# Where a graph network's second weight block is combined: beside the edge counting, or after the first head

## The chip, the cores and the metric

The kernel runs on one core of a Trainium2 chip. The core has a matrix engine (TensorE, PE in the profile), a vector engine (VectorE, DVE), an activation engine (ScalarE, ACT), a general engine (GpSimd, POOL) and a queue that starts transfers (SyncE, SP). Each engine runs its own instructions strictly in its own order; semaphores tie the engines together. Time is device microseconds of one execution, and the number compared is the median over executions: before the change 3097.74 us over three (3096.92 to 3099.75).

## The reference, cut to what matters

The model is a chain of four blocks over 512 nodes of width 768. Each block adds a graph layer, a token mixer and a feed-forward part to the nodes. Only the start of the first block is touched here: a layer norm, a count of the edges, and a graph attention layer with eight heads.

```python
edge_index = jnp.stack([src, dst])            # 16384 edges between 512 nodes
xn = _layernorm(x, axis=-1)                   # 512 x 768
# first graph layer, head by head (8 heads of 768 columns)
h = (x @ W).reshape(n, H, C)                  # W1 is 768 x 6144
alpha_s = jnp.einsum('nhc,hc->nh', h, a_s)
alpha_d = jnp.einsum('nhc,hc->nh', h, a_d)
e = jax.nn.leaky_relu(alpha_s[src] + alpha_d[dst], NEG_SLOPE)
m = jax.ops.segment_max(e, dst, num_segments=n)
e = jnp.exp(e - m[dst])
denom = jax.ops.segment_sum(e, dst, num_segments=n)
alpha = e / (denom[dst] + EPS)
out = jax.ops.segment_sum(h[src] * alpha[:, :, None], dst, num_segments=n)
# blocks 2 and 3 of the chain use the degree of each node
deg = jax.ops.segment_sum(jnp.ones_like(dst), dst, num_segments=n)
```

The second graph layer multiplies the eight heads' outputs by W2 (6144 x 768); the kernel does this head by head, as "project".

## The kernel before the change

**The edge counting.** Instead of gathering along edges, the kernel counts how often each pair of nodes occurs, in a 512 x 512 matrix `cnt`. `edge_counts` is a generator of 128 steps; step j takes 128 edges, makes a one-hot row block for their sources (512 wide) and one for their destinations (256 wide, the upper half of the nodes marked by a factor 4096), and multiplies them on PE into two PSUM banks (line 708, two matmuls a step). The source block comes from DVE (line 704, one instruction) or from ACT (lines 701 and 702, two instructions): for j below 40 every odd step is ACT's, from 40 on every third. The destination block is always DVE's (line 705). Its input is a row of node numbers. Up to step 31 that row is `near`, a copy in PSUM in 32-bit numbers; from step 32 on it is `nodes`, in SBUF in 16-bit numbers. The one-hots live in a ring of 16 buffers, so step j waits for the matmuls of step j - 16. The 128 steps fall into five groups; at the end of a group, ACT (714), DVE (716 to 721) and POOL (722, 723) split the two banks into counts and add them into `cnt`.

**The products.** Large products use a seven-multiplication scheme (Strassen-Winograd) over halves of both operands. It needs sums of the left operand and differences of the weights. `SplitB` makes the weight differences on POOL: for each of three chunks four subtractions of 128 x 384 (lines 438 to 441), twelve in all, two of which (439) overwrite a quarter of the weights themselves. A product over three chunks (line 512 in the profile, 128 x 384) is the unit of PE work; a head takes fourteen. A 32-bit matmul stands as two records in the trace, so a product is a row of six.

**The head loop.** `heads(i)` loads the 768 columns of W1 for head i (three transfers of 768 KB, `split_weights`), combines them (`SplitB`), makes h = xn @ W1 and then the two node scores on DVE (line 796, four instructions each). In the first head the counting runs as a background: at each product's start `tick()` puts in seven steps. For head 1 the combining is `pinned`: it is written so that it stays behind everything issued before it on its engine. From head 1 on the background is the edge weighing of the head before (`weighing`: line 743 to 763, then transposes, line 787), so that its aggregation (line 901, PE) can follow the head's products. After the aggregation comes `project`, with a block of W2 that is also combined on POOL.

**Order.** A scheduler places the instructions on the engines by what is ready in its own model; `pinned` steps and data hold it back. Weight blocks alternate between two buffers, their differences between two `tw` buffers. All transfers go through the one SP queue in order.

**The degrees.** `degrees` adds up the rows of `cnt` (line 928, one DVE reduction over 2048 numbers), and takes an inverse square root with one correction step (lines 929 to 936, six small instructions on DVE and one on ACT). It is called after head 2's turn in the loop, but not pinned, and its first use is far behind.

Of the kernel before, what the change touches and what calls it, by code (L numbers as in the profile page):

```python
# [19 lines left out]
N = 512  # L20
D = 768
# [76 lines left out]
def kernel(ctx: ExitStack, tc: tile.TileContext, a: dict, out: bass.AP):  # L98
    nc = tc.nc
    V, S, G, T = nc.vector, nc.scalar, nc.gpsimd, nc.tensor  # L100
# [278 lines left out]
    HT = N // 2  # L379
# [45 lines left out]
    def ready(src):  # L425

        return SplitB(split_weights(src))
# [242 lines left out]
    def edge_counts(gp):  # L670

        HI, MAGIC = 4096.0, 1.5 * 2.0 ** 23
        nodes = gp.tile([P, N], HF, name="nodes")
        G.iota(nodes, pattern=[[1, N]], base=0, channel_multiplier=0,
               allow_small_or_imprecise_dtypes=True)
        near = psum()[:, :HT]
        V.tensor_copy(near, nodes[:, :HT])
        part = gp.tile([P, 1], FP, name="part")  # L680
        G.memset(part, -31.0 / 64.0)
        ef = gp.tile([P, 2, EC], FP, name="ef")
        V.tensor_copy(ef, edges)
        neg = gp.tile([P, EC], FP, name="neg")
        V.tensor_scalar(neg, ef[:, 0, :], -1.0, None, op0=ALU.mult)
        far = gp.tile([P, EC], FP, name="far")
        V.tensor_scalar(far, ef[:, 1, :], float(HT), None, op0=ALU.is_ge)
        V.scalar_tensor_tensor(ef[:, 1, :], far, -float(HT), ef[:, 1, :], op0=ALU.mult, op1=ALU.add)
        V.tensor_scalar(far, far, HI - 1.0, 1.0, op0=ALU.mult, op1=ALU.add)
        hots = []  # L690
        for _ in range(2):
            b = big_tile("oh").bitcast(BF)
            hots += [b[:, i * (N + HT) : (i + 1) * (N + HT)] for i in range(8)]
        n_groups = -(-EC // 26)
        for g in range(n_groups):
            js = range(EC * g // n_groups, EC * (g + 1) // n_groups)
            acc = [psum() for _ in range(2)]
            for j in js:
                oh = hots[j % len(hots)]
                if (j % 2 if j < 40 else j % 3 == 2):  # L700
                    S.activation(oh[:, :N], nodes, AF.Abs, bias=neg[:, j : j + 1])
                    S.activation(oh[:, :N], oh[:, :N], AF.Relu, bias=1.0, scale=-1.0)
                else:
                    V.tensor_scalar(oh[:, :N], nodes, ef[:, 0, j : j + 1], None, op0=ALU.is_equal)
                V.tensor_scalar(oh[:, N:], near if j < 32 else nodes[:, :HT], ef[:, 1, j : j + 1], far[:, j : j + 1],
                                op0=ALU.is_equal, op1=ALU.mult)
                for u in range(2):
                    T.matmul(acc[u], oh[:, N + u * P : N + (u + 1) * P], oh[:, :N],
                             start=j == js[0], stop=j == js[-1])
                yield  # L710
            for u in range(2):
                low, high = cnt[:, u, :], cnt[:, 2 + u, :]
                t = gp.tile([P, N], FP, name="up_t", bufs=2)
                S.activation(t, acc[u], AF.Identity, bias=part, scale=1.0 / HI)
                if g == 0:
                    V.tensor_scalar(high, t, MAGIC, -MAGIC, op0=ALU.add, op1=ALU.add)
                    V.scalar_tensor_tensor(low, high, -HI, acc[u], op0=ALU.mult, op1=ALU.add)
                else:
                    V.tensor_scalar(t, t, MAGIC, -MAGIC, op0=ALU.add, op1=ALU.add)
                    r = gp.tile([P, N], FP, name="up_r", bufs=1)  # L720
                    V.scalar_tensor_tensor(r, t, -HI, acc[u], op0=ALU.mult, op1=ALU.add)
                    G.tensor_add(high, high, t)
                    G.tensor_add(low, low, r)
        for t in range(NT):
            S.activation(off[:, t, :], cnt[:, t, :], AF.Relu, bias=bigc, scale=-BIG)
        nc.sync.dma_start(cnt_dram, cnt)
# [89 lines left out]

    open_products()

    def heads(i):
        w1 = split_weights(a["L0_gnn_W1"][:, i * D : (i + 1) * D])  # L820
        B = pinned(lambda: SplitB(w1)) if i == 1 else SplitB(w1)
        h = token_major("h")
        strassen_token(xs, B, lambda t, c, ps: S.copy(h[:, t, ts(c, HC)], ps), None,
                       None if i else n0.rest)
        flush()
        return h, node_scores(h, row(f"g0_as{i}"), gp), node_scores(h, row(f"g0_ad{i}"), gp)

    with tc.tile_pool(name="graph", bufs=1) as gp:
        counting = edge_counts(gp)
        for _ in range(24):  # L830
            next(counting)
        n0 = Norm(x, "xn", 1e-5)
        for t in (0, 2, 1, 3):
            n0.chunk(t)
            if t == 1:
                n0.first()
        xs = n0.split
        raw_xn = tc.dram_tile([P, NT, D], FP, name="raw_xn")
        nc.sync.dma_start(raw_xn, n0.n)
        for _ in range(16):  # L840
            next(counting)
        background.append(several(counting, 7))
        loose.append(background[0])
        head0 = heads(0)
        drain()
# [46 lines left out]
    with tc.tile_pool(name="gat0", bufs=2) as gp:  # L892
        h2 = token_major("h2")

        def aggregate(i, h, wT, norm=None):
            gT = feature_major("gT")
            sums = SplitA(gT, G, False)
            for n, f in enumerate((0, 3, 1, 4, 2, 5)):
                ps = psum()
                for s in range(NT):  # L900
                    T.matmul(ps, h[:, s, ts(f, P)], wT[:, s, :], start=s == 0, stop=s == NT - 1)  # L901
                elu(gT[:, f, :], ps, col("g0_b1", i * KC + f))
                if norm and n < NT:
                    norm.chunk(n)
                if f >= KC // 2:
                    sums.sums(f - KC // 2)
            return sums

        def project(i, sums):
            first = set()  # L910

            def add(t, j, ps):
                d = h2[:, t, ts(j, HC)]
                if i == 0 and (t, j) not in first:
                    first.add((t, j))
                    evacuate(d, ps)
                else:
                    V.tensor_add(d, d, ps)

            strassen_add(sums, ready(a["L0_gnn_W2"][i * D : (i + 1) * D, :]), add)  # L920
            flush()


        dinv = const.tile([P, NT], FP, name="dinv")

        def degrees():
            deg = tiny(NT, name="deg")
            V.tensor_reduce(deg, cnt, AX.X, ALU.add)
            V.tensor_scalar(deg, deg, 1.0, None, op0=ALU.add)
            S.activation(dinv, deg, AF.Sqrt)  # L930
            V.reciprocal(dinv, dinv)
            nw = tiny(NT, name="ln_nw4")
            V.tensor_mul(nw, dinv, dinv)
            V.tensor_mul(nw, nw, deg)
            V.tensor_scalar(nw, nw, -0.5, 1.5, op0=ALU.mult, op1=ALU.add)
            V.tensor_mul(dinv, dinv, nw)

        done = None
        for i in range(9):
            if done:  # L940
                g, hg, ew = done
                wT = gp.tile([P, NT, N], FP, tag="edge_wT", name="edge_wT", bufs=wt_bufs[0])
                if i < 8:
                    if i == 1:
                        background.append(delayed(5, weighing(ew, s4, d4, cnt, off)))
                    background.append(delayed(0 if i == 1 else 8, turned(ew, wT)))
                else:
                    for _ in turned(ew, wT):
                        pass
            if i < 8:  # L950
                h, s4, d4 = heads(i) if i else head0
                drain()
            if done:
                norm = performer_norm() if i == 8 else None
                sums = aggregate(g, hg, wT, norm)
            if i < 8:
                done = i, h, edge_weights(s4, d4, gp, cnt, off) if i else weight_tile(gp)
            else:
                ys, va = performer_values(norm)
            if i:  # L960
                project(g, sums)
            if i == 2:
                degrees()
        x = load_x()
        qT = last_gat(h2, "g0_as", "g0_ad", gp, cnt, off, lambda: performer_features(ys, 0))
        add_row_to(x, row("g0_b2"))
# [903 lines left out]
    with tc.tile_pool(name="ffn3", bufs=1) as fp:  # L1870
# [83 lines left out]
        for g in range(2):  # L1954
            wa = weights(a["L3_ffn_w2a"][g * N : (g + 1) * N, :])
            wb = weights(a["L3_ffn_w2b"][g * N // 2 : (g + 1) * N // 2, :], HD)
            for i in range(2):
                j = 2 * g + i
# [94 lines left out]
```

## Time and profile before

| | us |
|---|---|
| median of 3 executions | 3097.74 (3096.92 to 3099.75) |
| the profiled execution | 3099.04 |
| its span, first to last instruction | 3097.2 |
| PE busy | 3005.4 (97%) |
| DVE busy | 1482.7 (48%) |
| POOL busy | 1436.3 (46%) |
| ACT busy | 749.7 (24%) |
| mean granted clock of TensorE | 0.992 |

The span is 1.8 us short of the profiled execution's own time, and that execution is 1.3 us above the median. PE is busy nearly all the time, so what a change at the start is worth must be read from the start: a busy share over 3 ms says nothing on it. In a timeline row the columns are start, duration, engine, line, operation and tiles, the number of instructions merged, and in brackets the idle time before them with what ended it. In a row of windows they are the stretch, its length, and the busy time of each engine with its number of instructions, then the clock granted to TensorE, the share of the transfer engines and GB/s.

### The profile page before, as it was taken

What the parts mean: (1) busy time and instruction counts of PE and PEld (TensorE: products, weight loads), DVE (VectorE), ACT (ScalarE), POOL (GpSimd) and SP (SyncE); (2) the same over time, 40 slices, a digit from 0 to 9 for tenths busy, and PEclk for the clock granted to TensorE, in tenths of its full rate; (3) what the DMA queues carried; (4) which work ended last, traced back from release to release, by engine and by line L of the source; (5) the groups of instructions that cost most, each with busy time, mean ns of one, the idle gap of its engine ahead of it and who ended that gap; (6) DMA issues with size and microseconds to landing.
All of it is one profiled execution on the core that took longest, in us unless ns stands there. A gap on an engine that the chain in (4) does not pass through costs nothing.

```text
span 3097.2 us, 31606 instructions
## 1 busy us (share of the span) xinstructions
PE 3005.4 (97%) x11757; PEld 2006.2 (65%) x11757; DVE 1482.7 (48%) x3416; ACT 749.7 (24%) x1434; POOL 1436.3 (46%) x1532
## 2 busy tenths in 40 slices
PE   7899999999999999999899999999999999999989
PEld 3455555556766777765675367877777776677755
DVE  9854444556256235446766435333333335462341
ACT  7322222252252112004432213100000012221111
POOL 3544444442516663655651444455544557355610
PEclk9999999999999999999999999999999999999999
DMA  3112212223202222321111512122221223122222
GB/s 116 56 70 72 72 72 72 71 92 82 82 1 97 92 92 93 118 92 57 61 72 62 148 67 97 67 92 92 92 90 68 88 92 123 60 89 77 99 80 62
DMA packets 92691, 253.63 MB, mean 82 GB/s; under 512 B 9889, under 2 KB 14881, under 8 KB 91514
## 3 DMA queue, kind: packets, MB, share of 16 engines
q1 hardware_dynamic: 92538, 251.61, 23.5%
q8 instruction: 93, 1.52, 0.2%
q14 instruction: 60, 0.49, 0.1%
HBM read 244.23 MB, written 7.36 MB: 81 GB/s over the span
## 4 chain that ended last, share of the span: by engine, by line
PE 86%; DVE 8%; POOL 2%; ACT 2%; issue 1%; DMA 0%; SPq 0%; POOLq 0%; ACTq 0%
PE ps L512 43%; PE ps L605 23%; PE ps L901 5%; PE ps L308 4%; PE ps L1109 1%; PE ps L1096 1%; PE ps L298 1%; PE ps L274 1%; PE ps L1934 1%; PE ps L1597 1%; POOL room L1455 1%; DVE edge_w L754 1%; DVE edge_w L743 1%; PE ps L1947 1%; PE ps L1324 1%
## 5 line engine op out<-in xcount | busy, mean ns | idle before, releaser
L438 POOL TENSOR_TENSOR tw<-w 128x384 f32<-128x384 f32 x246 | 247.8, 1017 | 953.4 <-DMA w<-in_L_gnn_W 308.1
L512 PE MATMUL ps<-sx,w 128*128 128x256 f32 x1188 | 316.9, 380 | 3.0 <-DVE sx L420 2.6
L512 PE MATMUL ps<-sx,tw 128*128 128x256 f32 x1188 | 290.3, 380 | 0.4
L605 PE MATMUL ps<-w,sx 128*128 128x384 f32 x720 | 256.4, 487 | 4.2 <-DVE sx L420 3.0
L440 POOL TENSOR_TENSOR tw<-w 128x384 f32<-128x384 f32 x246 | 254.0, 1039 | 9.6
L439 POOL TENSOR_TENSOR w<-w 128x384 f32<-128x384 f32 x246 | 252.7, 1036 | 8.8
L441 POOL TENSOR_TENSOR tw<-w,tw 128x384 f32<-128x384 f32 x246 | 251.7, 1030 | 10.3
L605 PE MATMUL ps<-tw,sx 128*128 128x384 f32 x720 | 250.5, 487 | 0.2 <-DVE x L654 0.2
L512 PEld LDWEIGHTS ps<-sx,w 128*128 128x128 f32 x1188 | 225.0, 190 | 38.2 <-PE ps L512 2.2
L512 PEld LDWEIGHTS ps<-sx,tw 128*128 128x128 f32 x1188 | 219.5, 190 | 43.0 <-DVE st_u L551 7.2
L527 ACT COPY st_p<-ps 128x256 f32<-128x256 f32 (+1 forms) x127 | 49.9, 394 | 722.1 <-PE ps L512 683.4
L551 DVE TENSOR_TENSOR st_u<-st_p,ps 128x256 f32<-128x256 f32 (+1 forms) x127 | 57.1, 450 | 346.7 <-PE ps L512 346.6
L605 PEld LDWEIGHTS ps<-tw,sx 128*128 128x128 f32 x720 | 136.0, 190 | 95.3 <-DVE x L1818 1.2
L605 PEld LDWEIGHTS ps<-w,sx 128*128 128x128 f32 x720 | 136.4, 190 | 94.3 <-POOL tw L441 4.1
L654 DVE TENSOR_TENSOR x<-x,ps 128x384 f32<-128x384 f32 x216 | 115.2, 552 | 164.1 <-PE ps L605 162.8
L512 PE MATMUL ps<-w,sx 128*128 128x384 f32 x456 | 170.3, 494 | 11.9 <-POOL w L439 10.1
L512 PE MATMUL ps<-xfT,w 128*128 128x256 f32 x720 | 176.8, 380 | 0.2
L512 PE MATMUL ps<-tw,sx 128*128 128x384 f32 x456 | 162.1, 491 | 4.9 <-DVE st_u L551 4.4
L901 PE MATMUL ps<-edge_wT,h 128*128 128x512 f32 x384 | 166.1, 592 | 0.0
L554 DVE TENSOR_TENSOR st_u<-st_p,ps 128x256 f32<-128x256 f32 (+1 forms) x127 | 57.1, 449 | 200.8 <-PE ps L512 200.8
L512 PEld LDWEIGHTS ps<-xfT,w 128*128 128x128 f32 x720 | 135.9, 190 | 24.1 <-issue 1.3
L605 PE MATMUL ps<-w,hid 128*128 128x384 f32 x432 | 142.9, 488 | 0.0
(484 smaller groups left out, 5063.6 us busy)
## 6 DMA issues: line engine op xcount, KB each, us to landing
w<-in_L_gnn_W SPq DMA_DIRECT2D x60, 768.0 KB, 6.8
w<-in_L_mix_fc_w SPq DMA_DIRECT2D x48, 768.0 KB, 6.3
row<-in_rows SPq DMA_DIRECT2D x39, 384.0 KB, 4.6
w<-in_L_mix_qkv_w SPq DMA_DIRECT2D x18, 768.0 KB, 5.2
w<-in_L_ffn_w SPq DMA_DIRECT2D x18, 768.0 KB, 7.0
w<-in_L_ffn_routed_gate SPq DMA_DIRECT2D x18, 768.0 KB, 5.9
w<-in_L_ffn_routed_up SPq DMA_DIRECT2D x18, 768.0 KB, 6.7
w<-in_L_ffn_routed_down SPq DMA_DIRECT2D x18, 768.0 KB, 5.7
```

The costliest lines, as they stand in the source:

```text
L308: T.matmul(ps, parts[k][:, ts(t, P)], w_of(k)[:, ts(c, HC)], start=k == 0, stop=k == n - 1)
L438: G.tensor_sub(tt[:, 0, k], b22[:, k], b12[:, k])
L439: G.tensor_sub(b12[:, k], b12[:, k], b11[:, k])
L440: G.tensor_sub(tt[:, 1, k], b22[:, k], b12[:, k])
L441: G.tensor_sub(tt[:, 2, k], b21[:, k], tt[:, 1, k])
L512: T.matmul(bank, l, r, start=start and k == 0, stop=stop and k == KC // 2 - 1, skip_group_check=True)
L527: S.copy(b["p1"], b["x"])
L551: V.tensor_add(b["u2"], b["p1r"], b["y"])
L554: V.tensor_add(u3, b["p1r"], b["y"])
L605: T.matmul(b[name], l[:, k, ts(m, P)], r[:, k, :], start=start and k == 0, stop=k == KC // 2 - 1, skip_group_check=True)
L654: V.tensor_add(x[:, t, ts(j, HC)], x[:, t, ts(j, HC)], ps)
L901: T.matmul(ps, h[:, s, ts(f, P)], wT[:, s, :], start=s == 0, stop=s == NT - 1)
```

## The change

Three edits. First, `heads` no longer makes its weights for heads 0 and 1: a list `first_two` is filled for both, load and combination, ahead of steps 24 to 39 of the counting, and head 1 takes its entry without `pinned`. Second, the destination one-hot reads `near` in PSUM up to step 39 instead of 31. Third, `degrees` is pinned where it is called. In the order of the built program POOL then has head 1's twelve subtractions directly behind head 0's twelve and before its first addition into `cnt`; on SP head 1's three transfers stand before the two score rows of head 0 instead of behind them, and the third transfer of the first W2 block stands behind the two score rows of head 1 instead of before them; the reduction of the degrees leaves its place between two of DVE's additions of head 0 and stands in front of head 3's first addition. On ACT the copy of head 1's first product (`st_p1`, line 527) changes places with the last copy of head 0's h.

```diff
-                V.tensor_scalar(oh[:, N:], near if j < 32 else nodes[:, :HT], ef[:, 1, j : j + 1], far[:, j : j + 1],
+                V.tensor_scalar(oh[:, N:], near if j < 40 else nodes[:, :HT], ef[:, 1, j : j + 1], far[:, j : j + 1],
                                 op0=ALU.is_equal, op1=ALU.mult)
...
+    def head_weights(i):
+        return ready(a["L0_gnn_W1"][:, i * D : (i + 1) * D])
+
     def heads(i):
-        w1 = split_weights(a["L0_gnn_W1"][:, i * D : (i + 1) * D])
-        B = pinned(lambda: SplitB(w1)) if i == 1 else SplitB(w1)
+        B = first_two.pop(0) if first_two else head_weights(i)
         h = token_major("h")
...
         nc.sync.dma_start(raw_xn, n0.n)
+        first_two = [head_weights(i) for i in range(2)]
         for _ in range(16):
             next(counting)
...
             if i == 2:
-                degrees()
+                pinned(degrees)
```

## The prediction

> **What bounds the kernel now.** I read the page first, then windows over the first 157 us, then what PE waited for, then the timelines of the engines in that stretch.
>
> ```profile
> PE 3005.4 (97%) x11757; PEld 2006.2 (65%) x11757; DVE 1482.7 (48%) x3416; ACT 749.7 (24%) x1434; POOL 1436.3 (46%) x1532
> ```
> ```profile
> 24.50:36.00 11.50, 7.67 (x30) 4.14 (x29) 11.07 (x45) 11.11 (x21) 1.03 (x2) 0.85 0.04 15
> 36.00:56.00 20.00, 17.39 (x74) 7.83 (x73) 19.70 (x59) 18.22 (x33) 5.30 (x4) 0.97 0.17 72
> 56.00:107.00 51.00, 50.54 (x205) 25.94 (x205) 45.16 (x133) 27.19 (x46) 10.38 (x8) 0.98 0.00 1
> 107.00:137.00 30.00, 19.21 (x50) 10.33 (x49) 21.67 (x31) 6.79 (x13) 27.77 (x22) 0.83 0.39 140
> ```
> ```profile
> PE ps L512 <- POOL w L439: 10.1, 2, 6.7
> ```
>
> Over the whole program PE is the bound (97%). The windows show where it is not. Up to 56 us DVE and ACT are full and PE is fed by them; from 56 to 107 PE itself is full (50.54 of 51.00), so a delay brought in before 56 is not won back there. From 107 to 137 PE works 19.21 of 30 us while POOL is full (27.77): PE stands for head 1's weight differences, 10.1 us in two waits. The timelines of PE, POOL and DVE show it:
>
> ```profile
> 111.22 2.10 PE L512 MATMUL ps<-w,xnT 128*128 128x384 f32 x6
> 116.75 1.65 PE L512 MATMUL ps<-w,sx 128*128 128x384 f32 x2 [3.43 <-POOL w L439]
> 118.19 2.87 PE L512 MATMUL ps<-w,xnT 128*128 128x384 f32 x6
> 128.41 1.65 PE L512 MATMUL ps<-w,sx 128*128 128x384 f32 x2 [6.72 <-POOL w L439]
> 129.86 3.85 PE L512 MATMUL ps<-tw,sx 128*128 128x384 f32 x6
> 134.35 2.20 PE L512 MATMUL ps<-tw,sx 128*128 128x384 f32 x6 [0.65 <-DVE st_u L551]
> 136.39 0.60 PE L329 MATMUL ps<-ident,ga_sc 128*128 128x128 f32 x4
> ```
> ```profile
> 24.61 1.00 POOL L441 TENSOR_TENSOR tw<-w,tw 128x384 f32<-128x384 f32 x1
> 48.44 1.31 POOL L722 TENSOR_TENSOR cnt<-cnt,up_t 128x512 f32<-128x512 f32 x1 [22.83 <-DVE up_t L719]
> ```
> ```profile
> 17.50 0.34 DVE L704 TENSOR_SCALAR oh<-nodes,ef 128x512 bf16<-128x512 f16 x1
> 17.76 0.98 DVE L705 TENSOR_SCALAR oh<-ps,ef,far 128x256 bf16<-128x256 f32 x2
> 37.20 0.60 DVE L705 TENSOR_SCALAR oh<-nodes,ef,far 128x256 bf16<-128x256 f16 x2
> 49.96 1.36 DVE L704 TENSOR_SCALAR oh<-nodes,ef 128x512 bf16<-128x512 f16 x1
> 51.24 1.28 DVE L705 TENSOR_SCALAR oh<-nodes,ef,far 128x256 bf16<-128x256 f16 x1
> 113.86 2.29 DVE L928 TENSOR_REDUCE deg<-cnt 128x4 f32<-128x2048 f32 x1 [1.77 <-POOL cnt L723]
> 117.44 1.74 DVE L796 SCALAR_TENSOR_TENSOR st_u<-h,row 128x768 bf16<-128x768 f32 x1
> ```
>
> POOL is idle for 22.83 us between head 0's last subtraction and the first addition into `cnt`: that is where head 1's twelve go. The DVE rows are the price list. Beside POOL's subtractions (up to 25.6) a 704 takes its usual 0.34 and a 705 from PSUM 0.98 for two; beside POOL's additions (49.7 to 52.4), back to back with 16-bit inputs from SBUF, 704 takes 1.36 and 705 takes 1.28 instead of 0.34 and 0.33.
>
> **Part 1, head 1's stall.** Before: from the start of its first product (111.22) to the transposes of head 0's scores (136.39) PE needs 25.2 us for five products. A product is 1.94 us (rows that follow without a gap stand that far apart), so 9.7 are work and 15.5 are lost: 10.8 idle (3.43, 6.72, 0.65), 4.2 in rows at about half speed (1.65 instead of 0.81 twice, 2.87 and 3.85 instead of 2.10), the rest gaps.
>
> After, on the same clock: first product until 113.2, a third of the next (0.65) until 113.8. Then PE needs ACT's copy of the first product (527), and that wait is new. It now stands behind the last copy of head 0's h, that one behind DVE's 560, and 560 behind the first node score (796). ACT gives the h that this score needs at 113.7 (row 823 at 113.26, 0.46), as before; the reduction at 113.86 is no longer in the way. So: score 0.87, 560 0.47, two copies of 0.48: PE goes on at 116.0, having lost 2.2. Two products and two thirds, 5.2, bring it to 121.2. There it needs 551, which stands on DVE behind the seven other scores: 115.1 + 7 x 0.87 = 121.2. The first W2 block, which is loaded once `cnt` is out (114.27), lands near 120 by its 5 to 7 us, and its subtractions can then meet the last two scores; a score beside them is 1.67 apart instead of 0.87. I take half of that, 0.8, and 551 itself: 122.3. One more product: the transposes stand at 124.2. Gain 136.39 - 124.2 = 12.2 us.
>
> [...] behind 2.60 us idle (at 27.84) six transposes take 1.51 us, behind 1.20 us (at 32.72) 0.88. By the row the product after the wait costs up to 1.0 more. PE then arrives at 122.2, still not after 551, so the sum is the same.
>
> Behind the transposes DVE's weighing of head 0 runs as before (743 to 763) and PE reaches line 787 with almost no slack (DVE's last scaling ends at 153.1, PE's transposes began at 152.57). The weighing starts 0.8 us sooner after the transposes, because the small degree instructions (134.2 to 137.3) are gone; POOL's W2 block reaches some 2 us further into it, its third chunk waiting for SP behind the score rows, which wait for the scores. I charge 0.3.
>
> **Part 2, the counting.** Eight 705s read PSUM instead of SBUF: from rows 17.76 and 37.20, starts are 0.45 and 0.25 apart, so 8 x 0.20 = 1.6 us on DVE. Twelve subtractions at 1.07 us run from 25.6 to 38.6 beside it. Four DVE instructions there fall outside the rhythm of one 704 and two 705s: two 704 (27.70, 29.13) and two 716 (30.60, 31.79), 32-bit SBUF to SBUF. None is seen beside a subtraction before, so bounds: nothing (row 17.50), or a whole subtraction, 1.0 each (row 49.96). I take half, 2.0. DVE waited 0.4 for ACT in that stretch, which takes some up. Sum 3.2 us, and it reaches PE where PE waits for DVE (52.58 to 55).
>
> [...] The trace has ten 704s beside POOL's first subtractions at 0.33 to 0.37, and POOL's instructions stretched from 0.99 to at most 1.21. I take the row for those in rhythm [...].
>
> **Part 3, what costs nothing.** Head 1's subtractions: the load is in time, since transfers fall silent at 23 us in the transfer view of the first 40 us; POOL has 22.83 us for 13. Without that cover they would hold up 722, and DVE behind it. The degrees at head 3: DVE has 7.45 us idle there (before 551 at 292.88). The reduction 2.3, ACT's table load and root 1.5, and six small ones with POOL beside them, up to 1 us each for three (0.43, 0.92, 0.84 at 134.87 to 136.49), come to some 7: 0, at most 1. A second table load falls before head 2's first exponential, where ACT has idle time (1.48 us at each row 802). The third W2 transfer: needed in `project`, 40 us later.
>
> **Sum:** -12.2 + 0.3 + 3.2 = -8.7 us. Against the profiled execution (3099.04, span 3097.2 and 1.8 around it) 3090.3; that one lies 1.3 above the median of the runs, so I forecast the median 3097.74 - 8.7 = **3089.0**.
>
> **Rivals.** *DVE takes POOL's place as head 1's bound* (0.17). In the old stretch 117 to 157 DVE is nearly full. If the W2 block's twelve subtractions each catch a score or a 754, 756 for 0.3 to 0.4 more than I charge, the aggregation starts some 4 us later: gain 4.7, 3093.0. For it: no slack at 787. Against: the same block met the same weighing before.
>
> *The subtractions hold up the counting as the additions do* (0.08). Place: DVE from 25.6 to 40. Price: rows 49.96 and 51.24, 1.0 us for each POOL instruction, twelve of them, and the 1.6: 13.6 against 11.9 won at head 1, so +1.7: 3099.4, slower. It decides from (11.9 - 1.6) / 12 = 0.86 us a subtraction. Half that rate gives -4.3, 3093.4. Against: row 17.50, and the 705s from PSUM leave POOL room.
>
> *The change does not do what it says* (0.02): a weight block late, or PSUM's bank held for `near` eight steps longer stops a product. No product in the built order waits for step 39, so I leave little: 3097.7.
>
> **How the numbers follow.** The main case has 0.73, with its own range from 3085.5 (no waits in the counting, the scores not met) to 3092. With the rivals, eight in ten lie between 3085 and 3095. This kernel can be told from no change from about 0.2%, 6.2 us, so faster means below 3091.5: most of the main case and a little of the first rival, 0.76; same 0.20; slower, the second rival with PE's clock falling besides, 0.04.
>
> **What would show it.** Right: POOL's twelve rows of 438 to 441 between 25.6 and 39; no wait of PE for 439 behind 107; a wait of about 2 us for ACT's 527; PE's first wait-free stretch beginning near 59 instead of 56; 796 at 0.95 instead of 1.74 for most of head 0; the reduction inside DVE's idle stretch before head 3. Wrong: 704 above 0.5 between 27 and 40, PE waiting over 1 us at 787, or PE's stretch beginning after 62.

## The result and the profile after

The changed kernel takes 3089.98 us (median of 7 runs, 3088.08 to 3091.6), the kernel before 3099.27 (7 runs, 3096.92 to 3101.06): ratio 0.997, 95% interval 0.9959 to 0.9982. That is 9.3 us less, where the forecast was 8.7 less; the forecast time, 3089.0, lies 1.0 under the measured one. The profiled execution has a span of 3088.8 us. A second set of runs of the same program, on another occasion, gave 3089.02 against 3099.66, ratio 0.9966 (0.9954 to 0.9979).

First come two windows over the same stretches as before (PE, PEld, DVE, ACT, POOL with instruction counts, then the granted clock, DMA share and GB/s), then what PE waited for between 100 and 160 us.

```profile
24.50:36.00 11.50, 7.46 (x25) 3.40 (x24) 11.50 (x40) 10.91 (x21) 10.87 (x12) 0.72 0.00 1
...
107.00:137.00 30.00, 27.09 (x84) 14.94 (x82) 21.09 (x43) 11.69 (x20) 17.35 (x16) 0.94 0.42 140
```
```profile
PE ps L512 <- ACT st_p L527: 2.2, 1, 2.2
```

Head 1's twelve subtractions now run on POOL from 25.24 to 38.03; the window from 24.5 to 36 has 10.87 us of POOL's work where it had 1.03. The window from 107 to 137 gives PE 27.09 us of work instead of 19.21. PE's two waits for line 439 are gone (439 overwrites weights in three of the twelve subtractions, one for each chunk), and the forecast wait for ACT's 527 is there, at 2.2. The timelines of POOL, DVE and PE show the steps one by one (start, duration, what, and in brackets the idle time before it and who ended it).

```profile
25.24 1.00 POOL L438 TENSOR_TENSOR tw<-w 128x384 f32<-128x384 f32 x1
37.01 1.02 POOL L441 TENSOR_TENSOR tw<-w,tw 128x384 f32<-128x384 f32 x1
...
122.90 0.99 POOL L438 TENSOR_TENSOR tw<-w 128x384 f32<-128x384 f32 x1 [7.49 <-DMA w<-in_L_gnn_W]
```
```profile
27.48 1.06 DVE L704 TENSOR_SCALAR oh<-nodes,ef 128x512 bf16<-128x512 f16 x1
29.68 0.90 DVE L704 TENSOR_SCALAR oh<-nodes,ef 128x512 bf16<-128x512 f16 x1
31.37 0.41 DVE L716 TENSOR_SCALAR cnt<-up_t 128x512 f32<-128x512 f32 x1
35.05 0.96 DVE L704 TENSOR_SCALAR oh<-nodes,ef 128x512 bf16<-128x512 f16 x1
36.84 0.34 DVE L704 TENSOR_SCALAR oh<-nodes,ef 128x512 bf16<-128x512 f16 x1
41.76 0.99 DVE L705 TENSOR_SCALAR oh<-ps,ef,far 128x256 bf16<-128x256 f32 x2
...
89.68 0.55 DVE L551 TENSOR_TENSOR st_u<-st_p,ps 128x384 f32<-128x384 f32 x1
...
115.33 0.96 DVE L796 SCALAR_TENSOR_TENSOR st_u<-h,row 128x768 bf16<-128x768 f32 x1 [1.67 <-ACT h L825]
...
276.55 2.28 DVE L931 TENSOR_REDUCE deg<-cnt 128x4 f32<-128x2048 f32 x1
...
284.01 0.55 DVE L551 TENSOR_TENSOR st_u<-st_p,ps 128x384 f32<-128x384 f32 x1 [1.48 <-PE ps L512]
```
```profile
90.29 2.20 PE L512 MATMUL ps<-tw,sx 128*128 128x384 f32 x6 [0.24 <-DVE st_u L551]
...
112.79 2.10 PE L512 MATMUL ps<-w,xnT 128*128 128x384 f32 x6
...
117.72 3.69 PE L512 MATMUL ps<-w,xnT 128*128 128x384 f32 x6 [2.19 <-ACT st_p L527]
121.20 1.71 PE L512 MATMUL ps<-w,sx 128*128 128x384 f32 x4
122.75 2.10 PE L512 MATMUL ps<-tw,sx 128*128 128x384 f32 x6
125.56 2.20 PE L512 MATMUL ps<-tw,sx 128*128 128x384 f32 x6 [0.72 <-DVE st_u L551]
127.60 0.60 PE L329 MATMUL ps<-ident,ga_sc 128*128 128x128 f32 x4
...
147.51 20.76 PE L904 MATMUL ps<-edge_wT,h 128*128 128x512 f32 x48
```

From the kernel before, PE's timeline and DVE's:

```profile
55.79 3.34 PE L512 MATMUL ps<-w,xnT 128*128 128x384 f32 x6
...
88.71 2.20 PE L512 MATMUL ps<-tw,sx 128*128 128x384 f32 x6 [0.46 <-DVE st_u L551]
...
156.30 20.76 PE L901 MATMUL ps<-edge_wT,h 128*128 128x512 f32 x48
```
```profile
88.12 0.54 DVE L551 TENSOR_TENSOR st_u<-st_p,ps 128x384 f32<-128x384 f32 x1
```

From head 1's first product to the transposes PE needs 127.60 - 112.79 = 14.8 us instead of 25.2. The product behind the 2.19 us wait runs at about half speed (3.69 for six; at full speed such a row behind a wait takes 2.20). The aggregation starts at 147.51 instead of 156.30, 8.8 us earlier, and the degrees (from 276.55, the last of the small ones at 282.37) fit ahead of the 551 at 284.01, with 1.48 us to spare.

How far one execution agrees with the next matters for all that follows. From 150 to 1395 us the two programs keep a constant distance; behind 1395 us PE has waits, and how fast the products behind them run differs from one execution to the next, by up to 2.5 us in all (experiments 1 and 9, one program, between 1395 and 1700 us). So below a stage is read from its own rows, and a time only where the difference is larger than that. Ahead of the counting's second half, too, PE's first transposes of the normalization (near 27.5 us) start up to 0.6 us apart from one execution to the next; "from the transposes at 27" means that this is taken out.

### The profile page after: what moved, and what is told of

Read it like the earlier page. It is cut to its first block, busy times and chain, and to the rows that moved or that the text cites. A ratio compares the mean times of both kernels' runs of the same rounds, so it can differ in the third digit from the quotient of the medians.

```text
span 3088.8 us, 31610 instructions
## 1 busy us (share of the span) xinstructions
PE 3004.2 (97%) x11757; PEld 2006.4 (65%) x11757; DVE 1481.0 (48%) x3416; ACT 753.1 (24%) x1436; POOL 1430.7 (46%) x1532
## 4 chain that ended last, share of the span: by engine, by line
PE 87%; DVE 9%; POOL 2%; ACT 1%; issue 1%; DMA 0%; SPq 0%; POOLq 0%; ACTq 0%; DVEq 0%
PE ps L512 43%; PE ps L605 23%; PE ps L904 5%; PE ps L308 4%; DVE oh L705 1%; PE ps L1112 1%; PE ps L1099 1%; PE ps L298 1%; PE ps L274 1%; PE ps L1937 1%; PE ps L1600 1%; POOL room L1458 1%; DVE edge_w L754 1%; PE ps L708 1%; DVE edge_w L743 1%
## 5 line engine op out<-in xcount | busy, mean ns | idle before, releaser
L441 POOL TENSOR_TENSOR tw<-w,tw 128x384 f32<-128x384 f32 x246 | 250.4, 1025 | 10.4
L605 PE MATMUL ps<-w,hid 128*128 128x384 f32 x432 | 142.9, 488 | 0.0
```

Source lines behind the costliest of these rows:

```text
L441: G.tensor_sub(tt[:, 2, k], b21[:, k], tt[:, 1, k])
L605: T.matmul(b[name], l[:, k, ts(m, P)], r[:, k, :], start=start and k == 0, stop=k == KC // 2 - 1, skip_group_check=True)
```

## The experiments

**1. The numbers from PSUM until step 32 only.**

```
-near if j < 40 else nodes[:, :HT]
+near if j < 32 else nodes[:, :HT]
```

> The changed kernel with the numbers from PSUM ended at step 32 again. The theory (the longer use of PSUM costs 0.2 us for each of eight second one-hots and hides nothing): in the changed kernel steps 32 to 39 start at 38.26 us, behind head 1's last subtraction (37.01 and 1.02), so nothing is left there to be in the way; DVE gains 8 x 0.2 = 1.6 us, PE's wait-free stretch starts near 57.3 instead of 58.91, and the time falls by 1.0 to 1.6, to about 3088.6. The rival (the numbers from PSUM keep DVE and POOL apart): 705 or 704 above 0.5 us at 37 to 42 and a time 1 to 4 us above that of the changed kernel.

```profile
111.08 2.10 PE L512 MATMUL ps<-w,xnT 128*128 128x384 f32 x6
...
116.01 2.20 PE L512 MATMUL ps<-w,xnT 128*128 128x384 f32 x6 [2.19 <-ACT st_p L527]
...
124.19 0.60 PE L329 MATMUL ps<-ident,ga_sc 128*128 128x128 f32 x4
```

From the transposes at 27 to head 1's first product it takes 83.51 us, the changed kernel 85.08, the kernel before 83.38. So beside numbers from PSUM until step 32 head 1's twelve subtractions cost the counting a net 0.1 us (0.4 in experiment 9), and the eight one-hots more from PSUM cost the rest, 1.6. The stage moved as the theory said. In the same trace the 2.19 us wait is followed by a product at full speed (2.20), and the transposes stand 13.11 us behind the first product instead of 14.81. The time did not follow: 3092.41 us (8 runs; ratio 0.9974, 0.9963 to 0.9984), 7.6 below the kernel before (3100.03 in these sets of runs), where the changed kernel was 9.3 and 10.6 below it. The two intervals overlap, so the medians alone don't separate the two programs. Experiments 9 to 11 ask why the time did not follow.

**2. The degrees not held.**

```
-                pinned(degrees)
+                degrees()
```

> The changed kernel with the degrees not held. They fall back in front of head 0's first score. The theory (the degrees matter only once POOL no longer sets head 1's start): the reduction waits for POOL's last addition (115.42), takes 2.3, and the eight scores follow from 118.3: PE waits about 4.5 us for ACT's copy 527 instead of 2.19, DVE's 551 comes 2.4 to 4.8 later (the lower end if no score meets the W2 block's subtractions, the upper if three do), and the time rises by 2.4 to 4.8, to 3092.4 to 3094.8. The rival (the gain is the weights' alone, the degrees are hidden): within 0.5 of the changed kernel.

Two views of this run, DVE's timeline and PE's:

```profile
114.80 2.29 DVE L931 TENSOR_REDUCE deg<-cnt 128x4 f32<-128x2048 f32 x1 [1.78 <-POOL cnt L723]
...
122.74 1.74 DVE L796 SCALAR_TENSOR_TENSOR st_u<-h,row 128x768 bf16<-128x768 f32 x1
```
```profile
115.94 2.20 PE L512 MATMUL ps<-w,xnT 128*128 128x384 f32 x6 [1.04 <-ACT st_p L527]
...
126.67 4.21 PE L512 MATMUL ps<-tw,sx 128*128 128x384 f32 x6 [5.30 <-DVE st_u L551]
```

3093.78 us (12 runs; ratio 0.9981, 0.9972 to 0.9989), and the aggregation 3.1 us later than in the changed kernel's first profile, where a product ran at half speed, and 4.8 later than in its second (experiment 5). The size is the theory's, the path is not: 527 now stands on ACT ahead of the last copies of h, so PE waits only 1.04 us for it, and the whole delay arrives at 551 (5.30 us), which stands on DVE behind the reduction and eight scores. The last two scores meet POOL's W2 block and take 1.74 and 1.73 instead of 0.95. Without the hold, part of what the early differences win is lost again: 6.25 us are left against the kernel before.

**3. The degrees alone held, in the kernel before.**

```
-                degrees()
+                pinned(degrees)
```

> The kernel before with the degrees alone held behind the third head. The theory (the degrees matter only where POOL no longer sets head 1's start): PE still waits for POOL's 439 twice, since those subtractions start behind the additions to the counts either way; head 0's transposes stand within 1 us of 136.39, the aggregation within 1 us of 156.30, and the time does not change by more than 1 us. The rival (the degrees are worth by themselves what they cost in the changed kernel without the hold, 3.9 us at the transposes): the transposes at 133 or earlier.

```profile
118.30 1.65 PE L512 MATMUL ps<-w,sx 128*128 128x384 f32 x2 [5.63 <-POOL w L439]
...
128.66 1.14 PE L512 MATMUL ps<-w,sx 128*128 128x384 f32 x2 [4.86 <-POOL w L439]
...
135.95 0.60 PE L329 MATMUL ps<-ident,ga_sc 128*128 128x128 f32 x4
```

3101.5 us (12 runs; ratio 1.0007, 0.9999 to 1.0015, which does not tell it from no change). PE waits 10.5 us for 439, as before (10.1), and the transposes stand at 135.95 against 136.39. By itself the hold is worth nothing at head 1: POOL sets that stage. Experiments 2 and 3 together show that it has a value (3 to 4.5 us) only behind the early differences. The median says less than the stage does: up to 1395 us this run is 0.4 ahead of the kernel before, and from 1900 us on it loses 3.0 us, in the same places as experiments 1, 9 and 10 below. What the early differences win with neither the hold nor the longer use of PSUM was not run.

**4. Work for PE in the 2.19 us wait.** Head 1's first product is followed by three products whose result is not used.

```
+        def fill():
+            ps = psum()[:, :n] if warm and fresh is None and warm.pop() else None
+            for k in range(3 if ps is not None else 0):
+                T.matmul(ps, ident, B.b11[:, k, :], start=True, stop=True, skip_group_check=True)
...
-                S.copy(b["p1"], b["x"])
+                S.copy(b["p1"], b["x"]); fill()
```

> The changed kernel with three products of 128x384 more, whose result is not used, in PE's order between head 1's first product and the one that waits for ACT's copy 527 (about 1.94 us of work into a wait of 2.19; the third of a product that stood there goes behind). The theory (the product after the wait is slow, 3.69 for six instead of 2.10, because PE stood idle for 2.19 us): the idle time falls to about 0.9, the product behind takes 2.10, head 0's 551 comes at about 123.4 instead of 124.95 and the transposes at about 126.1 instead of 127.6: 1.5 us less, 3088.5. The rival (it is slow for another reason, such as the scores or the copies beside it): the row stays near 3.7 and the time is that of the changed kernel or 0.6 above, for the third that was moved behind.

```profile
114.67 2.10 PE L502 MATMUL ps<-w,ident 128*128 128x384 f32 x6
117.66 2.20 PE L512 MATMUL ps<-w,xnT 128*128 128x384 f32 x6 [0.90 <-ACT st_p L527]
```

The product behind the shorter wait runs at full speed, and the transposes stand 13.76 us behind the first product, against 14.81: as the theory has it, 1.1 instead of 1.5 us. But experiments 1 and 5 have the unfilled wait with full speed behind it, at 13.11. So the filling shows no more than that a wait of 0.90 was harmless once; it costs 0.65 for the third that it moves behind. Time 3089.54 (5 runs; ratio 0.9968, 0.9955 to 0.998), no difference from the changed kernel.

**5. The changed kernel once more.**

> The changed kernel itself once more, on the same chip as these, to see how far one execution of the same program differs from another. Both theories: transposes between 125.7 and 127.6 (the product behind the 2.19 us wait at full or at half speed), and differences of up to 2 us from the first profile between 1395 us and the end, where PE has waits.

```profile
116.81 2.20 PE L512 MATMUL ps<-w,xnT 128*128 128x384 f32 x6 [2.18 <-ACT st_p L527]
...
125.00 0.60 PE L329 MATMUL ps<-ident,ga_sc 128*128 128x128 f32 x4
...
140.06 2.20 PE L512 MATMUL ps<-w,sx 128*128 128x384 f32 x6 [0.43 <-DVE ps L555]
```

The same instruction, the same wait, and now full speed: the clock granted from 107 to 137 is 1.00, where the first profile has 0.94. The transposes stand 13.11 us behind the first product (111.89). Of seven executions with this wait (2.18 or 2.19 us) five have full speed behind it and two half. The 1.7 us that this saves are not kept in full: with the transposes earlier, PE comes to a wait of 0.43 us for DVE's 555 inside the weighing, and the aggregation (145.82) is 20.82 us behind the transposes instead of 19.91.

**6. The mask's activations behind copy 527.**

```
-        for t in range(NT):
-            S.activation(off[:, t, :], cnt[:, t, :], AF.Relu, bias=bigc, scale=-BIG)
...
+    background.extend([delayed(1, offs()), delayed(3, weighing(ew, s4, d4, cnt, off))])
```

> The changed kernel with ACT's four activations that make the mask from the counts issued behind the copy 527 of head 1 instead of ahead of head 0's last two copies of h. The theory (ACT's activations, which wait for POOL's additions, hold up the first score, the copy of h and the copy 527 in turn): the first score starts at 113.7 instead of 115.33, 527 ends near 116, PE waits 0.5 instead of 2.19 us and does not slow down; the scores end near 121.2, 551 runs near 121.5, the transposes stand at 124.1 instead of 127.6: 3.5 us less, 3086.5. The rival (the weighing then meets more of the W2 block's subtractions, which start at 122.9 as before): the transposes at 124.1 but the aggregation only 1 to 2 us earlier than 147.51, 3088 to 3089.

PE's timeline, then DVE's:

```profile
116.13 2.20 PE L512 MATMUL ps<-w,xnT 128*128 128x384 f32 x6 [0.88 <-ACT st_p L527]
...
140.96 2.20 PE L512 MATMUL ps<-w,sx 128*128 128x384 f32 x6 [2.02 <-DVE ps L555]
```
```profile
130.96 2.67 DVE L754 SCALAR_TENSOR_TENSOR edge_w<-edge_w 128x512 f32<-128x512 f32 x2 [1.22 <-ACT edge_w L753]
...
136.38 2.07 DVE L754 SCALAR_TENSOR_TENSOR edge_w<-edge_w 128x512 f32<-128x512 f32 x2
```

The chain is nearly as described: PE waits 0.88 us for 527 instead of 0.5, and the transposes stand at 124.48, 11.98 us behind the first product. And the rival is right about what follows: two pairs of 754 that took 2.27 and 1.30 in the changed kernel take 2.67 and 2.07 beside the W2 block's subtractions, PE waits 2.02 us for 555, and the aggregation starts at 146.72, only 0.8 earlier than 147.51 and 0.9 later than in experiment 5. Time 3090.68 (6 runs; ratio 0.9972, 0.996 to 0.9983). Here DVE has taken POOL's place: earlier transposes alone hardly bring the aggregation forward.

**7. The W2 block held back as well.** Numbers from PSUM until 32, mask late, and the block's load waits for a DVE copy into its buffer (made behind half of the weighing). In a second version head 2's differences are also pinned behind the sums of gT.

```
+        V.tensor_copy(w[:, : KC // 2, 0], den[:, 1:2].to_broadcast([P, KC // 2]))
...
+        B = first_two.pop(0) if first_two else pinned(lambda: head_weights(i)) if i == 2 else head_weights(i)
```

The first line is in both versions, the block's three loads follow it; the last line is the second version's.

> The changed kernel with three edits: numbers from PSUM until step 32 only, the mask's activations behind copy 527, and the first W2 block's load held until DVE has half of head 0's weights (by a copy of three values into the block's buffer), so that its twelve subtractions come some 15 us later. The theory (in the run with the mask moved, DVE's weighing beside those subtractions took back what the transposes had won): head 1 starts near 111.1, the transposes stand near 123.0, no wait of PE for DVE's 555, the aggregation 19.9 later at 142.9, that is 4.6 us before the changed kernel's 147.51; the time near 3085.4. The rival (the held block pushes head 2's differences and the sums of gT back on POOL, and PE waits at the projection or at head 2): the aggregation at 142.9 but 2 to 5 us of it given back by 250 us.

> The run with the held W2 block once more, and head 2's twelve differences pinned behind the sums of gT on POOL. The theory (in that run the projection waited for the sums, 2.89, 3.68 and 1.98 us, only because head 2's differences stood ahead of them on POOL): no wait of PE for 410 at 168 to 182, the aggregation near 143.9, and from 250 to 1395 us a shift of about -3.6 us against the first profile of the changed kernel (-1.9 against the second); the time near 3087. The rival (those differences now meet DVE's weighing of head 1): 1 to 3 us given back by 250 us.

The first version's PE timeline, then the second's, then the second's DVE timeline:

```profile
143.93 20.76 PE L914 MATMUL ps<-edge_wT,h 128*128 128x512 f32 x48
...
171.89 0.91 PE L605 MATMUL ps<-w,sx 128*128 128x384 f32 x2 [2.89 <-POOL sx L410]
176.49 1.65 PE L605 MATMUL ps<-w,sx 128*128 128x384 f32 x2 [3.68 <-POOL sx L410]
180.11 1.65 PE L605 MATMUL ps<-w,sx 128*128 128x384 f32 x2 [1.98 <-POOL sx L410]
```
```profile
179.40 4.21 PE L605 MATMUL ps<-w,gT 128*128 128x384 f32 x6 [4.37 <-ACT h L205]
```
```profile
174.09 1.47 DVE L756 SCALAR_TENSOR_TENSOR edge_w<-edge_w,cnt 128x512 f32<-128x512 f32 x1
```

In both the aggregation starts near 144 (143.93 and 144.15), 3.4 to 3.6 us ahead of the changed kernel, one us short of the theory's 142.9. In both it is more than given back. In the first POOL makes head 2's differences ahead of the sums, and PE stands 8.6 us for the sums: 3099.07 us (13 runs; ratio 0.9997, 0.9989 to 1.0005). In the second, 3.4 us ahead at the aggregation and 3.1 behind at 200 us, the same differences meet head 1's weighing on DVE (a 756 takes 1.47 instead of 0.69), the copies of the projection come late, and PE stands 4.37 us for one of them and then runs at half speed (4.21 for six instead of 2.20): 3093.82 us (14 runs; ratio 0.9983, 0.9975 to 0.9991). In all these runs POOL's subtractions, wherever they were put, met DVE instructions of which some then took longer (a 704 1.06 us instead of 0.30 in the changed kernel, two 754 2.67 instead of 2.27 in experiment 6, a 756 1.47 instead of 0.69 here), and what it cost was decided by whether PE waited for those.

**8. The numbers from PSUM until step 16 only.** Now 16 of the second one-hots made beside POOL's subtractions read 16-bit numbers from SBUF.

```
-near if j < 40 else nodes[:, :HT]
+near if j < 16 else nodes[:, :HT]
```

> The changed kernel with the numbers from PSUM ended at step 16: 24 second one-hots more than in the changed kernel read SBUF, 16 of them while POOL makes head 0's and head 1's differences. Without any wait DVE gains 24 x 0.2 = 4.8 us. The theory (back to back with 16-bit inputs from SBUF each POOL subtraction holds DVE up by most of its length, as rows 51.96, 1.29, and 53.17, 1.37, show beside the additions): some 15 to 20 subtractions at 0.7 to 1.0 cost 10 to 18 us, PE's wait-free stretch starts 5 to 13 us later than 58.91, and the time rises as much. The rival (subtractions do not hold DVE up wherever it reads from): rows of 704 and 705 at 0.34 beside the subtractions, the stretch starts 3 to 5 us earlier.

```profile
20.79 1.10 DVE L704 TENSOR_SCALAR oh<-nodes,ef 128x512 bf16<-128x512 f16 x1
21.81 2.15 DVE L705 TENSOR_SCALAR oh<-nodes,ef,far 128x256 bf16<-128x256 f16 x2
...
42.01 0.59 DVE L705 TENSOR_SCALAR oh<-nodes,ef,far 128x256 bf16<-128x256 f16 x2
```

Beside subtractions a 704 takes up to 1.10 and two 705 take 2.15; without them (42.01) 0.59. So a one-hot beside a subtraction is held for 0.6 to 0.8 us; the fifteen held ones lose 10.7 us together, at the lower end of the expected 10 to 18 and under the 0.86 to 1.0 of the forecast's second rival. Head 1's first product is 3.1 us later than in the changed kernel, not 5 to 13: from the 10.7 go off the 4.8 that 24 one-hots win by reading SBUF and the 1.9 that the changed kernel's own one-hots wait, so DVE is 4.0 us later, and PE 3.1. Time 3093.21 (13 runs; ratio 0.998, 0.9972 to 0.9988). So the numbers in PSUM are what makes the subtractions cheap (one-hots wait 1.9 us in the changed kernel and 10.7 here), but only up to the step at which the subtractions end. That is step 32, not 40.

**9. Experiment 1 once more.**

> The changed kernel with the numbers from PSUM ended at step 32, run a second time. In its first profile it stood 2.46 us ahead of the changed kernel from 200 to 1395 us and 2.7 behind at the end, with slower products after the same waits of PE at 1421, 1487 and 2988 us. The theory (which of those waits is followed by slow products differs from execution to execution, and the earlier start is real): again ahead by 0.7 to 2.5 us at 1395, whatever the end is; the median near 3089 to 3091. The rival (the shift itself makes the later products slow): behind by 2 to 3 us at the end again, the median above 3092.

Head 1's first product stands 83.75 us from the transposes at 27, and until 1395 us the run is 2.5 us ahead of the changed kernel's first profile and 0.9 ahead of its second. The median is again 3092.34 (10 runs; ratio 0.9976, 0.9966 to 0.9985). From 1900 us to the end it loses 2.8 us in the same places as in its first profile; the changed kernel's two profiles differ there by 0.1. So the loss belongs to the program. But behind the counting the programs have the same instructions in the same order, and the trace has 3852 DVE instructions here (semaphore instructions counted) and 3850 in the changed kernel.

**10. Two more DVE instructions at the start of the changed kernel.**

```
+    for i in range(1): V.memset(sb[:, i : i + 1], 0.0)
```

The next instruction overwrites what this one writes; with its semaphore instruction it makes two.

> The changed kernel with one tiny write on DVE ahead of everything (128x1, overwritten at once), which with its semaphore instruction puts each later DVE instruction two places further back in DVE's instruction stream: 3733 DVE instructions instead of 3731, as many as the run with the numbers from PSUM ended at step 32 has. That run lost 2.8 us in the same places of both its profiles (0.2 at 1975, 0.2 at 2147, 0.5 at 2850, 1.0 at 2988, 0.5 at 3025 us and small ones between) although the program is the same there. The theory (those losses come with the place of DVE's instructions in the stream): the same places lose the same here, nothing differs before 1395 us, median near 3092. The rival (they came from something else that changed, such as the PSUM bank set free earlier): no loss in those places, median 3089 to 3090.

DVE's timeline of this run and of the changed kernel, at the same instruction, then PE's of this run and of the changed kernel, at a later one:

```profile
2846.64 0.42 DVE L551 TENSOR_TENSOR st_u<-st_p,ps 128x256 f32<-128x256 f32 x1 [5.06 <-PE ps L512]
```
```profile
2848.08 0.42 DVE L551 TENSOR_TENSOR st_u<-st_p,ps 128x256 f32<-128x256 f32 x1 [4.69 <-PE ps L512]
```
```profile
2986.88 3.65 PE L365 MATMUL ps<-xfT,rt_w 128*32 128x512 f32 x12
```
```profile
2988.24 2.46 PE L365 MATMUL ps<-xfT,rt_w 128*32 128x512 f32 x12
```

3091.98 us (10 runs; ratio 0.9977, 0.9968 to 0.9986). From 1900 us to the end it loses 2.5 us in the places named: 0.3 at 1975, 0.4 at 2850, 1.3 at 2988, 0.6 at 3025. At 1975 and 2850 DVE is late: it starts 551 0.35 and 0.37 us later after the same product. At 2988 and 3025 it is not: there PE, behind waits of the same length, runs slower (at 2988 the twelve matmuls take 3.65 instead of 2.46, at a granted clock of 0.58 instead of 1.00; ahead of 3025 forty-eight take 22.69 instead of 22.11). So about 0.7 of the 2.5 us are DVE's and 1.8 are PE's slower matmuls. The losses come as the theory said, in the same places, with two instructions of no work 2 to 3 ms ahead; how they come, it does not show. All four profiles with 3852 DVE instructions (experiments 1, 3, 9 and this one) lose 2.5 to 3.0 us there. The ten others change by 0.3 at most, whether they have fewer (3848, 3850) or more (3855, 3857), so it is no cost that grows with the number.

**11. The numbers from PSUM until step 35**, with as many DVE instructions as the changed kernel has.

> The changed kernel with the numbers from PSUM ended at step 35: five second one-hots fewer read PSUM, all behind head 1's last subtraction, and the program happens to have 3731 DVE instructions, as the changed kernel has. The theory (the longer use of PSUM costs 0.2 us each and hides nothing; later losses come with the place in DVE's stream): head 1's first product 0.5 to 1.0 us earlier than in the changed kernel, counted from PE's first transposes near 27.5, no loss behind 1900 us, median 3088 to 3089. The rival (PSUM's bank set free earlier costs the later 2.8 us): the same loss behind 1900 us as with step 32, median near 3092.

3088.97 us (8 runs; ratio to the kernel before 0.997, 0.996 to 0.9981). Head 1's first product is 83.51 us from the transposes at 27, and from 1900 us to the end nothing is lost (0.03). This version is 1.0 us ahead of the changed kernel's second profile at 1395 us; the medians, 3088.97 against 3089.98 and 3089.02, do not tell the two apart.

## Why the prediction was right

**Head 1's stall** (forecast -12.2, measured -10.4 in this profile and -12.1 in the second). Each row that it was built from is there: the first score waits for ACT's h (1.67 us), PE waits 2.19 us for 527, 551 runs behind the scores, the degrees are out of the way. The interval from the first product to the transposes was forecast as 124.2 - 111.22 = 13.0 us; it is 13.1 in five of seven executions. In the profile shown above it is 14.8, and there one step failed as it was put: "By the row the product after the wait costs up to 1.0 more. PE then arrives at 122.2, still not after 551, so the sum is the same." The product and the two thirds behind it cost 1.75 more than at full speed behind the same wait (3.69 - 2.20 and 1.71 - 1.45), so the price was above the "up to 1.0" as well; the scores ended at 122.83, and 551 stood waiting for PE until 124.95. The forecast had given the scores 0.8 us for meeting the W2 block; the block's first subtraction started at 122.90, just behind the last score, so that term was 0. Had the scores met it as assumed, 0.8 us of PE's delay would have been hidden. That 13.1 comes so near to 13.0 in the five others is in part luck: the 0.8 was missing there too, and in its place 551 with PE's restart took 0.88 us (122.08 to 122.96 in experiment 5) where the forecast had 0.3.

**The weighing behind the transposes** (forecast +0.3): 0.0 in this profile (19.91 us before and after), +0.9 in the second, where the transposes are earlier. That there is no slack was right, though PE's wait stands at 555 and not at 787: 0.43 us in experiment 5, 2.02 in experiment 6. These two show that the first rival's mechanism, DVE as the next bound, sets the limit from there. What a score that meets a subtraction pays was right for one score (1.74 instead of 0.95 in experiment 2, twice), but in the changed kernel none met one: the forecast's half stood for both cases.

**The counting** (forecast +3.2, measured +1.7 in this profile and +1.3 in the second). DVE's sum was right, and of its terms the one for PSUM: a 705 from PSUM is 0.45 from the next as forecast, eight of them 1.6 us. DVE waited 0.76, 0.55 and 0.62 us at three 704 (27.48, 29.68 and 35.05, against 0.30, 0.35 and 0.34 before), 1.9 in all, where the forecast had 2.0 for two 704 and two 716. That these agree is in part luck: the 716 did not wait (0.41 and 0.42), two of the 704 paid 1.3 where 1.0 was put, and the third, counted as in rhythm, paid 0.6. Less the 0.4 that DVE had waited for ACT there before, this put DVE back by 3.0 us between 23 us and step 40, against the forecast 3.2. One sign named for being wrong, a 704 above 0.5 between 27 and 40, did appear (1.06, 0.90 and 0.96), though the sum itself charged two such waits; the second rival, for which it was to stand, did not come.

What failed is the path: "it reaches PE where PE waits for DVE (52.58 to 55)". The wait that counts comes later. In the changed kernel DVE has no idle time from 24 to 90 us, and PE waits at 90.29 for a 551 on DVE, as it did at 88.71 before; that 551 starts 1.56 us later than before (89.68 and 88.12), and head 1's first product is 1.57 later. (At 23 us DVE was 0.3 ahead of the kernel before.) On the way to the 551 DVE has won back 1.1 of its 3.0 us, 0.5 of it from two waits for ACT that only the kernel before has (0.30 at 47.93 and 0.22 at 64.97); where the rest comes from was not taken apart. So the reading that PE itself bounds the stretch from 56 to 107 holds from 90 us on: up to there DVE sets the pace. Nor does a wait-free stretch of PE begin near 59 in the changed kernel: PE waits 1.46 us more at 79.01, for a 705, which costs nothing by 90.29. For the same reason the product at 55.79, at half speed in the kernel before (3.34 for six), cost it nothing: in experiment 1 the same product runs at full speed (2.10 at 55.77), and PE then waits 1.58 us for the 551 instead of 0.46. Experiments 1 and 9 put 0.1 to 0.4 of the loss on the subtractions and the rest on PSUM.

**The degrees** (forecast 0): 0; the room of 7.45 us was enough with 1.48 left.

Together, from the transposes at 27 to the aggregation: 119.8 us against 128.5, which is -8.7 (-10.4 + 1.7 + 0.0) in this profile; -9.9 (-12.1 + 1.3 + 0.9) in the second. That the first is the forecast to the decimal is chance: the stall's smaller gain (1.8 less, most of it the product at half speed) is made up by the smaller losses in the counting (1.5) and at the weighing (0.3).

**Waits of PE and waits of the one-hots.** Behind the 2.19 us wait the product ran at half speed in two executions of seven (3.69 and 3.90 for six instead of 2.20; in the first of them the granted clock from 117.72 to 121.13 is 0.58). Behind a wait of 3.26 us near 1425 us, the same instruction in fourteen profiles, six matmuls took 2.20 in four and 3.00 to 3.86 in ten. By the forecast's rows (six transposes in 1.51 us behind 2.60 us idle, in 0.88 behind 1.20) both waits would have cost speed each time: the length of the wait alone does not decide. What decides, the traces do not show.

In the changed kernel the 704s in rhythm with two 705 from PSUM did not wait at all (0.34 at 36.84), and those out of rhythm waited 0.55 to 0.76; in experiment 8, without PSUM, one-hots waited 0.6 to 0.8 us beside subtractions. The forecast's half of a subtraction for each of four instructions, 0.5 us, was its own estimate between two rows (17.50 and 49.96); of the four, the 704s waited 0.76 and 0.55, the two 716 not at all.

## What to carry to other kernels

Before you move work onto an idle engine, price it by the instructions that will run beside it: head 1's twelve subtractions cost PE 0.1 to 0.4 us beside one-hots that read PSUM; with one-hots that read SBUF, beside them and part of head 0's, PE lost 3.1 us; and head 2's, moved beside a head's weighing, gave back 6.5 us (experiment 7). When an engine stops being the bound, the next wait is already in the trace (here a reduction of 2.29 us ahead of the scores), so such an edit is worth nothing alone and 3 to 4.5 us behind another. A delay that meets a full engine goes on to the place where another engine next waits for it, so follow it there (here from DVE's steps before 40 to PE's wait at 90.29); the first wait on the way need not be the one that counts. Read a gain of a few us from the stage's own rows and in two executions, because elsewhere the same program, or a program with two more instructions, can move by as much.

## What was not expected of the hardware

Two more DVE instructions of no work at the start of the program made it lose 2.5 us 2 to 3 ms later, between 1900 us and the end (experiment 10). Four profiles of three programs with that number of DVE instructions (3852) lose 2.5 to 3.0 us there, in the same places; ten profiles with 3848, 3850, 3855 or 3857 lose or win 0.3 at most. At two of the places DVE starts one instruction 0.35 and 0.37 us later behind the same product, at two others PE runs slower behind the same waits (twelve matmuls in 3.65 instead of 2.46 us at 2988, the granted clock 0.58 instead of 1.00; forty-eight in 22.69 instead of 22.11 ahead of 3025). Why this number of instructions and not the others does it, the traces do not show.

PE's speed behind one and the same wait differs from one execution to the next: six matmuls took 3.69 or 3.90 us instead of 2.20 behind 2.19 us of idle time in two of seven executions (granted clock 0.58 in the changed kernel's first profile), 2.20 to 3.86 behind 3.26 us near 1425 us, and 2.20 or 3.81 to 3.90 behind 1.56 us near 1602 us (granted 0.56 for the 3.90). That spread alone moves a run by up to 1.7 us in each such place.
